# A convolution and attention kernel on one core: nine steps of the second image's statistics move from the fill into the first five periods, and two steps of offset arithmetic move ahead of a loop in the last period but one

## The chip, the core and the metric

The kernel runs on one core of one Trainium2 chip. A core has five engines, each with its own in-order queue of instructions: TensorE (PE, matrix products), VectorE (DVE), ScalarE (ACT), GpSimd (POOL) and SyncE (SP). [...] In this kernel SP issues most DMAs, POOL and ACT some. The metric is the device time of one execution in microseconds. The kernel before was run three times: 3306.95, 3310.23 and 3310.55 us, median 3310.23.

## What is computed

The input `x` has two images of 512 channels and 64 x 64 pixels. Two layers are applied, each of the form x + layer(groupnorm(x)), with 32 groups of 16 channels:

```
x = x + dcn(_gn(x))          # deformable convolution: offsets and mask from a depthwise
                             # 3x3 convolution, layer norm, Gelu and a product; bilinear
                             # sampling of a projected image; output projection
x = x + attention(_gn(x))    # q, k, v of all 4096 pixels, softmax, projection, batch norm, relu
```

The change is in the first layer. Its group norm needs mean and variance of every channel of an image before any pixel of that image can be normalized. Per image these are 32 statistics instructions (4 blocks of 128 channels, 8 pieces of 512 pixels), one aggregate for each block, and a short chain over the groups: product, differences, product, square root, reciprocal.

## The kernel before, in words

An image is cut into 8 chunks of 512 pixels (8 rows), and the two images make 16 chunks, 0 to 15. Each chunk passes through four stages, each written as a Python generator that issues some instructions and yields:

- `project` (L738): loads the chunk's rows, normalizes them on ACT (`xn`, L762), projects them on PE (`pq`, L772), and writes the result to DRAM (`xt`).
- `features` (L786): the depthwise convolution, 4 first taps on ACT (L798) and 32 taps on DVE (L806, about 0.7 us each), a sum over channels (`tot`, by POOL's DMAs and L816), the mean as a product (`p_mean`, L822), a subtraction (L827), squares on ACT (L832), the variance as a second product, the square root on ACT (`rstd`, L840), reciprocal and multiplication on DVE (L842, L843), and Gelu on ACT (L849).
- `weights` (L857): four pairs of a product `po` (L866) and an addition (L871), which are the first eight steps. Then, a step each: the exponential of the mask on ACT (L878); three operations on DVE that make `tx` from the offsets (L883, L884); a Relu on ACT (L890); the sums over the mask and its scaling on DVE (L893 to L898); the product `my` (L901); nine steps that add to `aw` (L909, L914); four copies to `at` on ACT (L919); and four transpositions `p_tr` with copies to `awT` (L928, L929).
- `sample` (L946): eight products `pb` with a copy to `bt` each (L957, L962), which for the last two chunks go to ACT and DVE by turns; eight groups of `pa` products with copies to `dT` (L976, L987); four output products `py` (L996), each followed by the residual's addition and a statistics instruction on DVE (L1001, L1002).

The order in which the four stages' steps are interleaved is written out by hand. Under `tc.manual_schedule()` each engine takes its instructions in the order in which the Python code issues them. First comes the fill, which brings chunks 0 to 2 under way: `p0`, `p1`, `p2` are their projections, `f0`, `f1`, `f` their features, and `v` the weights of chunk 0. Then come 16 periods. In period i, the function `period` (L1025) interleaves the end of the sampling of chunk i - 1 (`y`), the weights of chunk i + 1 (`w`), the sampling of chunk i (`m`), the features of chunk i + 2 (`f`, and `g` for the first step of the next) and the projection of chunk i + 3 (`p`); `v` is the tail of the weights of chunk i. `w(2)` issues two steps of `w`, and so on. Period 14 is `next_to_last`, period 15 `last_period`.

The statistics of the first image run at the very start. Those of the second are the generator `image_stats(1)` (L703), called `later`, and each `more()` issues one step of it. Its first step only issues three loads. Each of the next 32 steps issues, on POOL, the load of a piece two steps ahead (L714) and, on DVE, one statistics instruction (L727) on the piece that is due; after each eighth, an aggregate (L729) stands at the start of the next step. Five steps of the group norm follow (L598 to L616). The loads take turns in three pieces of memory, `early` (two) and `xraw` (one), so a load can be issued only when the statistics instruction three steps before the one that it feeds is done. Whatever is left is issued by `run(later)` ahead of period 5, which is the first to project a chunk of the second image.

Before the change, the fill calls `more()` 1, 6, 3 and 3 times and each period five times: once ahead of the features' taps and once after seven or so of their steps, once after the second of four groups of taps, once ahead of L842, and once at the end, after the last `aw` step. So the fill holds the first 12 statistics instructions, periods 0 to 3 hold five each, and period 4 and `run(later)` the group norm.

Of the kernel before, what the change touches and what calls it, by code (L numbers as in the profile page):

```python
# [533 lines left out]
@with_exitstack  # L534
def kernel(ctx: ExitStack, tc: tile.TileContext, t_in: dict, out: bass.AP):
    nc = tc.nc
    keep = ctx.enter_context(tc.tile_pool(name="keep", bufs=1))
    far = keep.tile([P, NSEQ], F32, name="far")
    sums = keep.tile([P, 2, 4 * G], F32, name="sums")
    nc.vector.memset(sums, 0.0)  # L540
    al = keep.tile([DQ, 2], F32, name="al_f")
    nc.gpsimd.dma_start(al[:, 0:1], t_in["L1_conv_align_w"])
    nc.vector.tensor_reduce(al[:, 1:2], al[:, 0:1], AX.X, ALU.max, apply_absolute_value=True)
    nc.vector.memset(al[:, 0:1], 1.0 / SCORE_MAX)
    beyond = keep.tile([1, 1], I32, name="beyond")
    again = window_path(tc, t_in, out, far, sums, al, beyond)

    with tc.If(again > 0):  # L550
        general_path(tc, t_in, out)
# [3 lines left out]
def window_path(  # L555
# [70 lines left out]
    with ExitStack() as l0:  # L626
# [68 lines left out]
        def border():  # L695
            for n in range(NB):
                for e in (0, 1, WIN - 2, WIN - 1):
                    nc.sync.dma_start(xt_d[n][e], edge[:WIN, :])
                    nc.sync.dma_start(xt_d[n][2 : H + 2, e, :], edge[:H, :])
# [234 lines left out]
        def fetch(i, s):  # L934

            if i >= NSEQ:
                return
            n, ch = divmod(i, NCH)
            t = io.tile([P, PX, C], F32, name="patch", bufs=2)
            for p in range(PX):  # L940
                nc.sync.dma_start(
                    t[:SN, p, :], xt_d[n][ch * ROWS + PR * s : ch * ROWS + PR * s + SY, PC * p : PC * p + SX, :]
                )
            patches[i, s] = t
# [61 lines left out]
        def run(*generators):  # L1006
            for gen in generators:
                for _ in gen:
                    pass
# [15 lines left out]
        def period(y, v, m, w, f, g, p, more, last, ahead, taps):  # L1025

            p()
            y()
            v(4)
            more()
            f(ahead)
            more()
            y()
            for k, count in enumerate(taps):
                m(2)
                w()  # L1040
                f(count)
                w()
                if k == 1:
                    more()
            w()
            m()
            w()
            m()
            f()
            y()  # L1050
            f()
            m()
            p()
            w(2)
            f()
            y(2)
            w()
            m()
            p()
            f()  # L1060
            w(2)
            p()
            y(2)
            more()
            f()
            y()
            m()
            p()
            for k, steps in enumerate((1, 2, 4, 0)):
                p()  # L1070
                w(steps)
                if k == 0:
                    if last:
                        m(3)
                    f()
                p()
                if k == 2:
                    more()
                if k < 3 and not last:
                    m()  # L1080
                if k == 0:
                    f()
                if k == 2:
                    g()
                    w(4)

        def next_to_last(y, v, m, w):

            y(3)
            w(8)  # L1090
            v(4)
            for steps, tiles in ((1, 2), (1, 2), (2, 1), (1, 0)):
                m(2)
                w(steps)
                y(tiles)
            for _ in range(4):
                m(2)
                w(2)
            w(5)
# [24 lines left out]
        def value_weights():  # L1124

            for cb in range(KB):
                pw = ps.tile([P, C], F32, tag="mm", name="pw")
                for kb in range(KB):
                    nc.tensor.matmul(
                        pw, wv[:, kb, cb * P : (cb + 1) * P], wf[kb], start=(kb == 0), stop=(kb == KB - 1)  # L1130
                    )
                t = io.tile([P, C], F32, tag="xj", name="wc_part", bufs=2)
                nc.scalar.copy(t, pw)
                nc.sync.dma_start(wc_d[:, cb, :], t)
                yield

        def output_bias():
            pb = ps.tile([P, C], F32, tag="mm", name="p_bias")
            for cb in range(KB):
                for kb in range(KB):  # L1140
                    nc.tensor.matmul(
                        pb[:, cb : cb + 1], out_w[:, kb, cb * P : (cb + 1) * P], in_b[:, kb : kb + 1],
                        start=(kb == 0), stop=(kb == KB - 1),
                    )
            nc.vector.tensor_add(out_b, out_b, pb[:, :KB])
            yield
# [4 lines left out]
        def more():  # L1151
            next(later, None)

        with tc.manual_schedule():

            p0, p1, p2 = [Chain(project, i) for i in range(3)]
            f0, f1, v, products = Chain(features, 0), Chain(features, 1), Chain(weights, 0), value_weights()
            p0()
            for kb in range(KB):
                p0()  # L1160
                f0()
            for t in range(4):
                p0(2)
                f0(8)
            border()
            more()
            p1()
            for kb in range(KB):
                p1()
                f1()  # L1170
                if kb == 1:
                    next(products)
                    next(products)
            f0()
            f1(5)
            p1(4)
            f0()
            f1(11)
            f0()
            for _ in range(6):  # L1180
                more()
            p1(4)
            f0(3)
            f1(16)
            next(products)
            fetch(0, 0)
            fetch(0, 1)
            p2()
            v(4)
            for _ in range(3):  # L1190
                more()
            f1()
            v(2)
            f1()
            v(2)
            p2(4)
            v()
            f1()
            v()
            f()  # L1200
            for _ in range(3):
                more()
            v(3)
            p2(4)
            f1()
            v(4)
            f1(2)
            v(5)
            p2(4)
            next(products)  # L1210
            run(output_bias())
            f(6)
            v(4)
            for i in range(NSEQ):
                if i == NCH - 3:
                    run(later)
                    for k, name in enumerate(("wkT", "wqT", "wkT")):
                        nc.sync.dma_start(wkq[:, :, k, :], t_in[name].rearrange("(kb p) m -> p kb m", p=P))
                    for h in range(2):
                        nc.sync.dma_start(al[h * DQ : (h + 1) * DQ, :], t_in["L1_conv_align_w"])  # L1220
                w, m, g = Chain(weights, i + 1), Chain(sample, i), Chain(features, i + 3)
                if i + 2 >= NSEQ:
                    (next_to_last if i + 1 < NSEQ else last_period)(y, v, m, w)
                    y, v = m, w
                    continue
                ahead, taps = (7, (9, 7, 6, 6)) if i else (0, (7, 7, 6, 6))
                period(y, v, m, w, f, g, Chain(project, i + 3), more, i + 3 == NSEQ, ahead, taps)
                y, v, f = m, w, g
            y.rest()
# [820 lines left out]
```

## Time and profile before

| | |
|---|---|
| median of three runs | 3310.23 us |
| the profiled execution | 3315.49 us |
| its span, first to last instruction | 3313.6 us |
| mean granted TensorE clock | 0.983 |
| VectorE's statistics instructions L727 (64, both images) | 0.674 to 0.696 us each |
| POOL's loads L714 for the second image | 256 KB each, 0.54 to 0.91 us of POOL, 2.9 to 6.9 us from issue to landing (those after 100 us) |
| first output product `py` of chunks 0, 1, 2, 3, 4 | 206.38, 273.6, 339.9, 405.68, 471.54 us |
| first output product of chunks 13, 14, 15 | 1054.74, 1112.27, 1153.38 us |

The second layer starts at 1168.17 us with its first product on PE. How to read the lines that the prediction shows: a timeline line has the start and the length in microseconds, the engine, the line of the kernel, the operation, what it writes and reads, the shapes, how many instructions were merged, and in brackets how long the engine had been idle before it and what ended that. The chain of waits is followed back from the last instruction: at each step to what released it, or to the instruction before it on its engine; its lines have start, length and what it was. An idle time counts only where its engine is on that chain.

### The profile page before, as it was taken

The numbers are of one execution on the slowest core, as the hardware profiler recorded it, in microseconds if no ns is written. First come the engines' busy times: TensorE is split into PE (matmuls) and PEld (weight loads), VectorE is DVE, ScalarE is ACT, GpSimd is POOL, SyncE is SP. The second block draws the span as 40 slices with busy tenths as digits, with TensorE's granted clock in tenths as the row PEclk, the third lists the DMA queues.
The fourth block names the chain that finished last, engine by engine and source line by source line (L and its number), as shares of the span: only waits on it lengthen the run. The fifth ranks groups of instructions, "written<-read, shape, count | busy, mean of one in ns | idle before, by whom it ended". The sixth has DMA issues, their size and how long they took to land.

```text
span 3313.6 us, 38405 instructions
## 1 busy us (share of the span) xinstructions
PE 3154.1 (95%) x14207; PEld 2264.5 (68%) x14207; DVE 2729.4 (82%) x3907; ACT 1343.0 (41%) x1848; POOL 292.0 (9%) x420
## 2 busy tenths in 40 slices
PE   4899999999999899999999999999999999999993
PEld 2455556555655667787787877887777787787782
DVE  7999999999998678995876977968897796886875
ACT  2678887888786533203113112023311202203114
POOL 1100000000000001001001011000001101001022
PEclk9999999999999999999999999999999999999997
DMA  6345443444343368748657677657677758648689
GB/s 238 120 117 155 151 129 109 137 146 118 109 136 124 115 236 282 220 154 242 189 174 212 197 203 204 199 185 251 226 213 200 205 181 234 199 160 238 194 320 373
DMA packets 241236, 629.06 MB, mean 190 GB/s; under 512 B 28528, under 2 KB 45552, under 8 KB 240016
## 3 DMA queue, kind: packets, MB, share of 16 engines
q1 hardware_dynamic: 177952, 413.37, 37.8%
q0 software_dynamic: 51936, 179.86, 20.7%
q10 hardware_dynamic: 11152, 33.30, 2.7%
q8 instruction: 114, 1.87, 0.2%
q14 instruction: 82, 0.67, 0.1%
HBM read 406.61 MB, written 124.91 MB: 160 GB/s over the span
## 4 chain that ended last, share of the span: by engine, by line
PE 79%; DVE 10%; ACT 5%; DMA 3%; issue 1%; SPq 1%; POOL 0%; ACTq 0%; POOLq 0%; DVEq 0%
PE accy L1572 21%; PE accx L1572 16%; PE pa L976 7%; PE py L996 6%; PE pS L1454 6%; PE pq L772 6%; PE po L866 4%; PE pvy L1809 3%; PE pvx L1809 2%; PE pk L1890 2%; PE pb L957 2%; ACT bt L962 1%; DMA tot<-e 1%; DVE conv L806 1%; PE p_mean L822 1%
## 5 line engine op out<-in xcount | busy, mean ns | idle before, releaser
L1572 PE MATMUL accy<-tt,v 128*128 128x256 f32 x1944 | 579.0, 379 | 0.7 <-DVE ct L1638 0.6
L1459 ACT ACTIVATE e<-pS 128x1024 f32<-128x1024 f32 x256 | 248.6, 1021 | 748.5 <-PE pS L1454 744.2
L1572 PE MATMUL accx<-e,v 128*128 128x256 f32 x1728 | 453.3, 385 | 0.0
L1572 PE MATMUL accy<-e,v 128*128 128x256 f32 x1728 | 443.4, 379 | 0.0
L1572 PEld LDWEIGHTS accy<-tt,v 128*128 128x128 f32 x1944 | 368.7, 190 | 53.3 <-DVE tt L1530 2.2
L806 DVE SCALAR_TENSOR_TENSOR conv<-xn,L_conv_dw_w_sb,conv 128x504 f32<-128x504 f32 (+1 forms) x512 | 376.7, 744 | 30.5 <-ACT conv L798 14.7
L1572 PEld LDWEIGHTS accx<-e,v 128*128 128x128 f32 x1728 | 320.5, 190 | 116.3 <-issue 77.4
L1572 PEld LDWEIGHTS accy<-e,v 128*128 128x128 f32 x1728 | 328.3, 190 | 44.6
L1530 DVE TENSOR_TENSOR tt<-tt,e 128x512 f32<-128x512 f32 x432 | 298.8, 692 | 14.8
L1572 PE MATMUL accx<-tt,v 128*128 128x256 f32 x972 | 289.4, 379 | 1.3 <-DVE tt L1529 1.3
L1529 DVE TENSOR_TENSOR tt<-e 128x256 f32<-128x256 f32 x432 | 180.7, 418 | 133.0 <-PE accy L1572 131.0
L976 PEld LDWEIGHTS pa<-bt,patch 96*128 96x128 f32 x2048 | 248.3, 195 | 57.1 <-issue 39.2
L976 PE MATMUL pa<-bt,patch 96*128 96x128 f32 x2048 | 252.3, 280 | 7.5 <-issue 4.0
L1454 PE MATMUL pS<-q,keys 64*128 64x512 f32 x1024 | 255.5, 616 | 1.1 <-DVE vform L1827 0.8
L962 ACT COPY bt<-pb 96x1024 f32<-96x1024 f32 x120 | 226.0, 2024 | 52.6 <-PE pb L957 52.6
L772 PE MATMUL pq<-in_w,xn 128*128 128x512 f32 x512 | 234.1, 600 | 3.5 <-ACT xn L762 3.5
L996 PE MATMUL py<-dT,L_conv_out_w_sb 128*128 128x512 f32 x512 | 230.0, 593 | 0.0
L1577 ACT COPY u<-accx 128x256 f32<-128x256 f32 x54 | 20.1, 372 | 474.5 <-PE accx L1572 471.7
L866 PE MATMUL po<-om_w_pg,feat 128*128 128x432 f32 x512 | 210.3, 557 | 0.8 <-ACT feat L849 0.8
L987 ACT COPY dT<-pa 32x256 f32<-32x256 f32 x496 | 179.9, 363 | 67.8 <-PE pa L976 59.0
L1572 PEld LDWEIGHTS accx<-tt,v 128*128 128x128 f32 x972 | 184.4, 190 | 27.6 <-DVE tt L1529 2.5
L996 PEld LDWEIGHTS py<-dT,L_conv_out_w_sb 128*128 128x128 f32 x512 | 95.5, 190 | 114.3 <-issue 107.6
(289 smaller groups left out, 4386.7 us busy)
## 6 DMA issues: line engine op xcount, KB each, us to landing
v<-wv SPq DMA_DIRECT2D x420, 448.0 KB
tot<-e POOLq DMA_DIRECT2D x160, 512.0 KB, 6.8
patch<-xt SPq DMA_DIRECT2D x256, 192.0 KB
wv<-vform SPq DMA_DIRECT2D x48, 512.0 KB
v<-ww SPq DMA_DIRECT2D x54, 448.0 KB
wv<-vsum SPq DMA_DIRECT2D x48, 384.0 KB
xt<-xj SPq DMA_DIRECT2D x128, 128.0 KB
res<-in_x SPq DMA_DIRECT2D x64, 256.0 KB
```

What stands on the lines that cost most here:

```text
L772: nc.tensor.matmul(pq, xn[:, kb, 1 + 2 * t : 3 + 2 * t, :].rearrange("p r c -> p (r c)"), in_w[:, kb, :], start=(kb == 0), stop=(kb == KB ...
L806: nc.vector.scalar_tensor_tensor(dst, src, wt, dst, ALU.mult, ALU.add)
L866: nc.tensor.matmul(po[:, : 3 * GP], f[:, kb, t * P : (t + 1) * P], om_w[:, kb].rearrange("p a k g -> p (a k g)"), start=(kb == 0), stop=(k ...
L962: copy(bt[:SN].rearrange("s g q d -> s d (g q)")[:, d0 : d0 + 4, :], pb[:SN])
L976: nc.tensor.matmul(pa[:, p], xp[:SN, p, cb * P : (cb + 1) * P], bt[:SN, 4 * cb : 4 * cb + 4, PX * s + p, :], start=True, stop=True,)
L987: copy(dst, src)
L996: nc.tensor.matmul(py, out_w[:, kb, cb * P : (cb + 1) * P], dT[:, kb, :], start=(kb == 0), stop=(kb == KB - 1))
L1454: nc.tensor.matmul(p[:, a, :], keys[r, i, (2 * u + h) * P : (2 * u + h + 1) * P], c.q[r, qh, :], start=True, stop=True,)
L1459: nc.scalar.activation(e.rearrange("p a q -> p (a q)"), p.rearrange("p a q -> p (a q)"), AF.Exp)
L1529: nc.vector.tensor_sub(t[:, 0], x[:, 1], x[:, 3])
L1530: nc.vector.tensor_add(t[:, 1:3], t[:, 0].unsqueeze(1).to_broadcast([P, 2, HQ]), x[:, 0:3:2])
L1572: nc.tensor.matmul(out, v[:, blk, :], op, start=(first and g == 0), stop=(final and g == NG))
```

## The change

In the fill, the six and the first three calls of `more()` are taken out; one before and three late in the fill stay. In `period`, a second call stands directly behind the first, ahead of the taps, and a second one directly behind that after the second group of taps. So the fill issues the first load step and 3 statistics instructions, the 35 calls of periods 0 to 4 issue the rest, and `run(later)` finds nothing left.

In `next_to_last`, the two steps of `w` that are the exponential and the `tx` operations are issued ahead of the loop over `m`, and the loop's third round issues none instead of two; the number of steps issued by the end of the loop is the same.

```
@@ period
             y()
             v(4)
             more()
+            more()
             f(ahead)
             more()
             y()
...
                 f(count)
                 w()
                 if k == 1:
+                    more()
                     more()
             w()
             m()
@@ next_to_last
             y(3)
             w(8)
             v(4)
-            for steps, tiles in ((1, 2), (1, 2), (2, 1), (1, 0)):
+            w(2)
+            for steps, tiles in ((1, 2), (1, 2), (0, 1), (1, 0)):
                 m(2)
                 w(steps)
                 y(tiles)
@@ the fill
             f0()
             f1(11)
             f0()
-            for _ in range(6):
-                more()
             p1(4)
             f0(3)
             f1(16)
...
             p2()
             v(4)
-            for _ in range(3):
-                more()
             f1()
             v(2)
             f1()
```

More of the change, by code (lines that the diff above doesn't have):

```diff
@@ L1034, in period @@
             more()
+            more()
             f(ahead)
@@ L1043, in period @@
                 if k == 1:
+                    more()
                     more()
@@ L1091, in next_to_last @@
             v(4)
-            for steps, tiles in ((1, 2), (1, 2), (2, 1), (1, 0)):
+            w(2)
+            for steps, tiles in ((1, 2), (1, 2), (0, 1), (1, 0)):
                 m(2)
@@ L1179, in window_path @@
             f0()
-            for _ in range(6):
-                more()
             p1(4)
@@ L1189, in window_path @@
             v(4)
-            for _ in range(3):
-                more()
             f1()
```

## The prediction

> **What bounds the kernel now.** I read the profiled execution top down: the page's busy times and chain, then the chain of waits in order of time for the three places that the change touches (the fill before about 143 us, periods 0 to 4 up to 471.5 us, the last period but one after 1054.7 us), then the timelines of single engines. "Period k" runs from where the last ends to its own end, by the first `py` product: 206.4, 273.6, 339.9, 405.7 and 471.5 us end periods 0 to 4.
>
> ```profile
> PE 3154.1 (95%) x14207; PEld 2264.5 (68%) x14207; DVE 2729.4 (82%) x3907; ACT 1343.0 (41%) x1848; POOL 292.0 (9%) x420
> PE 79%; DVE 10%; ACT 5%; DMA 3%; issue 1%; SPq 1%; POOL 0%; ACTq 0%; POOLq 0%; DVEq 0%
> ```
>
> TensorE carries four fifths of the chain. Whatever moves work on VectorE pays only where VectorE is in the other fifth. In the fill, the chain reads (start, us, what):
>
> ```profile
> 71.88 4.94 DMA wvfc<-wc_part
> 78.71 5.87 PE p_mean L822 x8
> 84.58 6.87 PE pq L772 x16
> 91.44 3.45 PE pw L1129 x8
> 94.92 3.49 ACT feat L849 x3
> ...
> 102.41 3.43 PE p_mean L822 x8
> 105.84 2.91 PE po L866 x8
> 108.75 0.02 issue
> 108.78 0.61 DVE o L871
> ```
>
> No `gn_st` is in it, although six stand on VectorE from 77.39 to 85.97 and three from 104.75 to 107.16. VectorE's timeline says why:
>
> ```profile
> 85.28 0.69 DVE L727 BATCH_NORM_STATS2 gn_st<-xraw 128x6 f32<-128x512 f32 x1 [1.44 <-DMA xraw<-in_x]
> 85.89 3.34 DVE L842 RECIPROCAL rstd<-rstd 128x512 f32<-128x512 f32 x1
> ...
> 108.78 0.61 DVE L871 TENSOR_TENSOR o<-po,om_b_pg 128x432 f32<-128x432 f32 x1 [1.61 <-PE po L866]
> ```
>
> The reciprocal at 85.89 needs ScalarE's `rstd`, written at 84.61 to 85.30; the three statistics ahead of 108.78 end 1.61 us before the product that is waited for. In period 0 and again in period 2 the chain does hold a statistic:
>
> ```profile
> 147.17 1.20 DVE gn_st L727 x2
> ```
> ```profile
> 292.09 0.69 DVE gn_st L727
> ```
>
> There VectorE is the bound, and TensorE waits at the mean (0.43 us at 170.71, 3.65 at 180.80, 0.37 at 303.06):
>
> ```profile
> 303.06 1.13 PE L822 MATMUL p_mean<-tot,ones_c 128*128 128x512 f32 x2 [0.37 <-DVE tot L816]
> ```
>
> **Part one, out of the fill.** Nine statistics go (0.684 us each, 0.60 start to start), with nine POOL loads of 256 KB (0.54 us of issue each) and one aggregate (0.37). The first six gone, the reciprocal starts at 85.35 instead of 85.89. But the Gelu behind it starts at 93.42 after a table load at 92.13, and that stands behind a ScalarE copy at 91.53 which waits for TensorE's `pq`; the reciprocal's successor L843 ended at 91.55, so 0.5 us earlier is no gain. The three at 104.75 only lengthen the wait of 1.61 us. If this cover were gone, VectorE would give back 9 x 0.60 + 4.64 us of DMA waits (2.79, 0.41, 1.44) = 10.0 us. I take 0, because the chain passes neither group; the bounds are 0 and -10.0. SP's queue is not passed by any of these loads.
>
> **Part one, into periods 0 to 4.** Each period gets a second step ahead of its taps and a second one after the second group of taps. In steps: 7 instead of 5 statistics in periods 0 to 3, one instead of none in period 4, where the group norm's steps follow.
>
> Period 0: VectorE has no idle time from 142.5 us to the subtraction at 174.02, where ScalarE's squares wait for it (1.55 us) and carry the chain on to 189.75. Both statistics are ahead: +2 x 0.60 = +1.2 us.
>
> Period 1: the first extra one falls into waits (0.64 for ScalarE's `conv` at 205.51, 0.82 for `py` at 210.01); the second eats from 1.45 us by which VectorE was early for the mean (TensorE free at 237.11, the total done at 235.66). TensorE stays +1.2; VectorE leaves at +1.8.
>
> Period 2: +0.60 ahead of the taps less the wait of 0.82 us for `py` at 277.28 (TensorE itself is +1.2 by then), then +0.60: without more, the total is +2.2 late, and as TensorE already waits 0.37 there, so is TensorE. But there is a new wait. The loads rotate through three pieces, so a statistic's load is issued only when the third before it is done. The steps now stand as last-of-period, first, second, four taps, third: the third's load starts behind the last-of-period's end and has about 4.25 us (two statistics at 0.60, four taps in 3.1). POOL issues 0.3 us after that end (271.45 + 0.68, issue at 272.43), and such loads took 4.5, 4.3 and 6.4 us from issue to landing at 204.57, 272.43 and 339.42:
>
> ```profile
> 339.42 0.54 POOL L714 DMA_DIRECT2D xraw<-in_x  x1 [18.00 <-DVE gn_st L727]
> ```
>
> The wait is 0.3 + (4.3 to 6.4) - 4.25 = 0.4 to 2.5 us each time; taps, residual add and the two taps groups stand behind it on VectorE, and the mean on TensorE waits for those. I take the middle, 1.4 in period 2 (period 1's has 4.5 and is covered by the `py` wait). TensorE: about +3.6 after period 2. Without the load's wait +2.2; with the long landing +4.6.
>
> Period 3: the wait for `py` is only 0.19 us (343.50) and the slack at the mean 0.08 (368.83 against 368.90). So 1.2 + a load wait of about 2.0 comes through nearly whole: TensorE +6.6 (bounds +3.1 and +8.2, by the same steps with no waits and with 6.4 us landings).
>
> Period 4: one statistic (0.60) goes into the `py` wait of 1.03 at 409.31. The norm's second product, which in the kernel before stood a step later (at 450.26), now directly follows the step that computes its operand, in TensorE's order ahead of the third group of `pb`:
>
> ```profile
> 421.72 1.13 PE L957 MATMUL pb<-awT,sel 25*96 25x256 f32 x16
> ```
> ```profile
> 424.11 0.16 DVE L604 TENSOR_TENSOR gn_d<-gn_d 128x4 f32<-128x4 f32 x1
> ```
>
> VectorE reaches that operand at 424.27, behind seven taps; TensorE would stand from 421.72: +2.6 us, and behind it `pb`, with ScalarE's copies waiting for it. TensorE has no other wait in the rest of the period that this could replace (0.23 us of slack at the mean). The norm's square root moves from the period's end (table load 1.28 and 1.10 us of waiting at 467.16) to beside the other square root at 449.87; TensorE had no gap after it, so 0.
>
> Clock: a short wait can cost more than itself. The windows show the granted clock at 0.50 from 1238 to 1242 us after a gap of 2.21 us at 1237.78, and at 0.91 in 540 to 560, in a period of 67.3 us (537.07 to 604.40) beside 65.5 (471.54 to 537.07) with the same waits of 0.83 and 0.46 to 0.48. So a dip costs about 1.7 us. Gaps of 1.76 and more were followed by one each time that I looked (1088.44, 1136.48, 1237.78); the 0.89 at 1168.17 was not. The 2.6 us in period 4 gets one: +1.7. Those at the mean in periods 2 and 3 may (0 to 1.7 each); a dip lost by a shift would be -1.7.
>
> [...]
>
> Part one: +6.6 + 2.6 + 1.7 = +10.9 us.
>
> **Part two, the last period but one.** The exponential and the three `tx` operations move ahead of the loop. The tx operations (2.8 us) fall into VectorE's wait of 3.18 us before 1077.21. The exponential on ScalarE then stands ahead of the first `bt` copy: its table load and 0.68 us end near 1077.9, that copy ends 0.8 us later, at 1079.9, before the next `pb` at 1080.66 needs its bank. Then every later VectorE step advances one place, and the third round has none:
>
> ```profile
> 1089.51 1.12 DVE L893 TENSOR_REDUCE sx<-o 128x64 f32<-128x576 f32 x1
> ...
> 1093.46 1.85 DVE L962 COPY bt<-pb 96x1024 f32<-96x1024 f32 x1
> ```
> ```profile
> 1095.41 17.03 PE L976 MATMUL pa<-bt,patch 96*128 96x128 f32 x128 [3.96 <-issue]
> ```
>
> TensorE stands 3.96 us until the last copy of `bt` ends (1095.31). With the sums (2.6 us) one round earlier, that copy starts when its `pb` is done, 1090.8 to 1091.5, and `pa` at 1092.75 to 1093.45: -2.0 to -2.7 us. I take -2.0, as the clock is at 0.50 there from 1090 on. What follows is bound by `pa` and passes it on.
>
> **Sum.** +10.9 - 2.0 = about +8 to +9; I take +8, a little under, as the dip's chance is not 1. The profiled execution took 3315.49 us (span 3313.6 and 1.9 around it), 5.3 over the median of 3310.23; on it the sum gives 3323.5, on the median 3318. Ends of this case: no load waits and no dips, 3.1 + 2.6 - 2.7 = +3.0; long landings and two dips, 8.2 + 2.6 + 3.4 - 2.0 = +12.2. A measurement here can tell about 0.2%, 6.6 us.
>
> **Rivals.**
> *The periods hide it.* TensorE's periods without these statistics (65.5 us) are as long as those with five (65.8), which speaks for spare VectorE time; the slacks of 0.08 and -0.31 at the mean speak against. Only part two and half of the wait in period 4 would be left: -2.0 to +0.6, about 3309.5.
> *The fill is VectorE's after all* (faster). VectorE is at 90% in it, and 10.0 us leave; it needs the copy of `xj` at 91.53 to come earlier than `pq` allows. With the periods hiding theirs: -12, 3298. It decides from 6.6 us of the 12.
> *The POOL queue spreads the delay.* Every added load stands on the queue that also carries `tot` accumulations (3.3 us to landing); the total at 302.32 has some 2 us left. If two periods lose 2 to 3 us there on top: +14 or more, 3326.
>
> **How the numbers follow.** Forecast 0.65 (its ends +3.0 and +12.2 are 3313.2 and 3322.4; the bound 3310.23 + 6.6 = 3316.8 leaves 5.6 of these 9.2 us, 0.6, above it), hidden 0.17, faster fill 0.10, POOL 0.08. Slower: 0.65 x 0.6 + 0.08 = 0.47; faster 0.10; same, the rest, 0.43. The range leaves out the fill's and POOL's cases: 3307 to 3323.
>
> **What would show it.** Right: `gn_st` alone at 115 us in the fill and the `at` copies at the same 142.7 us; the mean of period 0 some 1.2 us later; VectorE waiting for `early` or `xraw` ahead of the third statistic; a TensorE wait of about 2.6 us for `gn_d`; `pa` two us closer to its `pb` in the last period but one. Wrong: `at` copies well before 142.7, or means that come on time in periods 2 and 3.

## The result, and the profile after

The changed kernel takes 3323.32 us (median of six runs, 3321.33 to 3329.76), the kernel before 3310.39 (six runs, 3306.95 to 3313.31). The ratio is 1.0037, with an interval from 1.0028 to 1.0047, so 9 to 16 us slower. The prediction said 3318, slower, in a range from 3307 to 3323: the sign came out, and the mechanism in the main; the size was too small, with the measured time at the range's upper end.

The profiled execution of the changed kernel took 3322.75 us with a span of 3320.7. The page's first lines:

```profile
PE 3152.9 (95%) x14207; PEld 2265.5 (68%) x14207; DVE 2729.9 (82%) x3907; ACT 1341.7 (40%) x1847; POOL 292.4 (9%) x420
PE 72%; DVE 12%; DMA 6%; ACT 4%; issue 4%; SPq 1%; POOL 0%; ACTq 0%; POOLq 0%; DVEq 0%
```

The engines are as busy as before. What changed is the chain: TensorE's share fell from 79 to 72%, and DMA rose from 3 to 6%. The table sets the profiled executions side by side, period by period (us, from one chunk's first `py` to the next; the first row is the start of the first `p_tr`). The three columns on the right are experiments that are told below.

| | before | after | part one alone | norm apart | late instead |
|---|---|---|---|---|---|
| fill | 143.68 | 143.29 | 143.55 | 142.50 | 142.80 |
| period 0 (from `p_tr`) | 62.70 | 63.74 | 63.25 | 63.76 | 63.19 |
| period 1 | 67.26 | 66.41 | 66.41 | 66.40 | 66.40 |
| period 2 | 66.22 | 69.31 | 70.56 | 69.76 | 67.12 |
| period 3 | 65.82 | 69.01 | 68.29 | 69.12 | 67.25 |
| period 4 | 65.86 | 71.46 | 68.46 | 65.66 | 65.90 |
| periods 5 to 13, with dips of the clock | 583.2 | 578.1 | 583.2 | 583.3 | 578.2 |
| period 14 | 57.53 | 56.07 | 57.55 | 56.29 | 56.13 |

A dip of the granted clock (to 0.50, for 3.41 us in these periods) makes an otherwise equal period 1.4 to 1.7 us longer (67.3 instead of 65.6 in most). The profiled execution of before had one in period 1 and four in periods 6 to 13, that of after one there. Mainly for that reason the two spans lie only 7.1 us apart, and the medians 12.9.

In the fill next to nothing is gained: in the four executions with the changed fill it ends at 142.50 to 143.55 us, in the two with the fill of before (one is the second part alone, told below) at 143.68 and 143.95. VectorE's timeline of the changed kernel, where the nine statistics are gone:

```profile
84.78 3.36 DVE L842 RECIPROCAL rstd<-rstd 128x512 f32<-128x512 f32 x1 [7.40 <-ACT rstd L840]
...
108.23 0.61 DVE L871 TENSOR_TENSOR o<-po,om_b_pg 128x432 f32<-128x432 f32 x1 [4.48 <-PE po L866]
```

What was work is now waiting. The reciprocal starts when `rstd` is there, and the addition when its product is, as before.

In period 0 TensorE now waits 1.62 us at the mean, where it waited 0.43 before (the first line is the kernel before):

```profile
170.71 1.13 PE L822 MATMUL p_mean<-tot,ones_c 128*128 128x512 f32 x2 [0.43 <-DVE tot L816]
```
```profile
171.36 1.13 PE L822 MATMUL p_mean<-tot,ones_c 128*128 128x512 f32 x2 [1.62 <-DVE tot L816]
```

In the periods the chain of waits now names the moved steps and their loads (start, us, what):

```profile
146.63 1.79 DVE gn_st L727 x3
...
159.88 1.19 DVE gn_st L727 x2
```
```profile
273.39 5.97 DMA early<-in_x
...
342.30 6.06 DMA xraw<-in_x
```

VectorE waits for a load, in front of the residual's addition, in periods 2 and 3 (2.11 and 1.66 us):

```profile
279.38 0.69 DVE L727 BATCH_NORM_STATS2 gn_st<-early 128x6 f32<-128x512 f32 x1 [2.11 <-DMA early<-in_x]
279.99 0.73 DVE L1001 SCALAR_TENSOR_TENSOR res<-py,L_conv_out_b_sb,res 128x512 f32<-128x512 f32 x1
...
348.38 0.69 DVE L727 BATCH_NORM_STATS2 gn_st<-xraw 128x6 f32<-128x512 f32 x1 [1.66 <-DMA xraw<-in_x]
```

and TensorE waits for that addition (2.44 us in period 2, 2.14 in period 3), then in period 4 for the norm's operand:

```profile
280.78 0.66 PE L928 MATMUL p_tr<-ident,at 128*128 128x128 f32 x4 [2.44 <-DVE res L1001]
...
349.79 0.66 PE L928 MATMUL p_tr<-ident,at 128*128 128x128 f32 x4 [2.14 <-DVE res L1001]
```
```profile
430.40 0.59 PE L607 MATMUL gn_p<-gn_d,gmat_sb 128*128 128x4 f32 x2 [2.54 <-DVE gn_d L604]
430.92 2.05 PE L957 MATMUL pb<-awT,sel 25*96 25x256 f32 x16
432.90 5.11 PE L866 MATMUL po<-om_w_pg,feat 128*128 128x432 f32 x8
```

The `po` group behind the wait took 5.11 us instead of 3.17: the clock was halved there, from 430.03 to 436.86 us (third column from the end: the granted clock):

```profile
430.03:436.86 6.83, 6.46 (x24) 3.59 (x25) 4.58 (x8) 3.71 (x2) 0.86 (x1) 0.50 0.22 38
436.86:440.27 3.41, 3.41 (x24) 1.69 (x23) 2.15 (x4) 1.18 (x1) 0.00 (x0) 1.00 0.00 0
```

In period 14 the gap ahead of `pa` went from 3.96 to 2.01 us:

```profile
1100.08 17.45 PE L976 MATMUL pa<-bt,patch 96*128 96x128 f32 x128 [2.01 <-issue]
```

### The profile page after: what moved, and what is told of

It is laid out like the page before. It is cut to its first block, busy times and chain, and to the rows that moved or that the text cites. A ratio compares the mean times of both kernels' runs of the same rounds, so it can differ in the third digit from the quotient of the medians.

```text
span 3320.7 us, 38410 instructions
## 1 busy us (share of the span) xinstructions
PE 3152.9 (95%) x14207; PEld 2265.5 (68%) x14207; DVE 2729.9 (82%) x3907; ACT 1341.7 (40%) x1847; POOL 292.4 (9%) x420
## 4 chain that ended last, share of the span: by engine, by line
PE 72%; DVE 12%; DMA 6%; ACT 4%; issue 4%; SPq 1%; POOL 0%; ACTq 0%; POOLq 0%; DVEq 0%
PE accy L1571 21%; PE accx L1571 16%; PE pS L1453 6%; PE pa L976 6%; PE py L996 6%; PE pq L772 5%; PE po L866 3%; DVE conv L806 3%; PE pvy L1808 2%; PE pvx L1808 2%; PE pk L1889 2%; DMA tot<-e 2%; PE pb L957 1%; ACT bt L962 1%; DVE tt L1529 1%
```

## The experiments

My theory was: the fill hides what is taken out of it, periods 0 to 3 lose by VectorE's load and by waits for loads, period 4 by one product that stands right behind its operand, and period 14 gains 2 us. The rivals were that VectorE's load alone makes the periods long, that the fill gains, and that period 14's gain is lost later. The prediction also had a rival in POOL's queue, where the added loads delay the partial sums of `tot`. It needs no run of its own: the third of these DMAs took 3.24 to 3.29 us to land in periods 0 to 4 of the kernel before and 3.27 to 3.38 in the changed one, and in neither does VectorE wait for them ahead of the total (L816). Each ratio is to the kernel before, run on the same chip.

**The second part alone.**

```
-            for steps, tiles in ((1, 2), (1, 2), (2, 1), (1, 0)):
+            w(2)
+            for steps, tiles in ((1, 2), (1, 2), (0, 1), (1, 0)):
```

> The kernel before with the second part of the change alone (the exponential and the tx steps ahead of the loop in period 14). By my theory the last copy of bt is made earlier and TensorE's gap ahead of pa shrinks from 3.96 to about 2.0 us, and the second layer passes that on: 2.0 us less than before, 3308.4 us, ratio 0.9994. By the rival, that something later (the second layer's first loads) takes it back: 1.000. If it cost time on ScalarE: above 1.0005.

Measured: 1.0000 (0.9991 to 1.0009). The gap ahead of `pa` is 2.01 us here too, and period 14 takes 56.28 us instead of 57.53:

```profile
1086.64 17.81 PE L976 MATMUL pa<-bt,patch 96*128 96x128 f32 x128 [2.01 <-issue]
```

So the trace shows 1.3 us and the times can't tell 1.3 us from none. Of the 1.95 us that the gap lost, the `pa` group gave some back: it runs 0.8 us longer (17.81 instead of 17.03), as more of it falls under the halved clock (6.5 instead of 4.9 us). No cost on ScalarE shows in the period. Nor does a later place take the gain back, as far as the traces tell: from the end of period 14 to the end of the span, the five executions with the second part take 2201.0 to 2203.3 us, the three without it 2201.3 to 2204.7.

**The first part alone**: the changed kernel with that loop as before.

> The changed kernel with period 14 as before, so the moved statistics alone. By my theory nothing is gained in the fill (its end, the first p_tr, within 0.6 us of 143.7) and periods 0 to 4 lose about 1.0, 0.7, 3, 3 and 5.6 us: 13 to 15 us above before, about 3324 us, ratio 1.0042. By the rival, that the fill gains and a part of the loss comes from period 14: under 1.0030.

Measured: 1.0042 (1.0028 to 1.0055), 3324.97 us. The loss is that of the moved steps; by the times, none of it comes from period 14. This run also prices the wait in period 4 by itself, since the clock did not dip behind it:

```profile
430.70 0.39 PE L607 MATMUL gn_p<-gn_d,gmat_sb 128*128 128x4 f32 x2 [2.52 <-DVE gn_d L604]
431.02 1.13 PE L957 MATMUL pb<-awT,sel 25*96 25x256 f32 x16
432.08 3.17 PE L866 MATMUL po<-om_w_pg,feat 128*128 128x432 f32 x8
```

The windows from 420 to 440 us of the changed kernel and of this one (the granted clock again third from the end):

```profile
420.00:440.00 20.00, 17.00 (x75) 8.54 (x75) 16.17 (x26) 11.92 (x7) 2.30 (x3) 0.83 0.36 101
```
```profile
420.00:440.00 20.00, 17.00 (x81) 8.52 (x79) 19.09 (x31) 15.00 (x9) 2.30 (x3) 1.00 0.38 106
```

Period 4 takes 68.46 us here, 2.6 over the 65.86 of before: the wait itself. With the dip it takes 71.46, 3.0 more: that dip lasted 6.83 us, where those of periods 2 and 3 lasted 3.41. Period 2 lost more here (70.56), with a wait of 3.35 us for its load.

**The norm's product apart from its operand.**

```
-                if k == 1:
-                    more()
+                if k in (1, 2):
                     more()
```

> The changed kernel with the second of the two steps after the second group of taps moved behind the third group, in all periods, so that in period 4 the norm's second product no longer stands right behind its operand; periods 0 to 3 have as many statistics ahead of the mean as in the changed kernel. By my theory TensorE's wait of 2.54 us for gn_d and the dip of the clock behind it go: period 4 takes 66 to 67.5 us instead of 71.5, the kernel 4 to 5.5 us less than the changed one, about 3318.5 us, ratio 1.0025. By the rival, that VectorE's load makes period 4 long, it stays at 70 us or more and the ratio at 1.0037.

Measured: 1.0018 (1.0009 to 1.0027), 3317.42 us; the changed kernel's interval, 1.0028 to 1.0047, lies just above this one. Period 4 is back at 65.66 us, with its statistics and the norm still in it, and the product no longer waits:

```profile
428.65 3.17 PE L866 MATMUL po<-om_w_pg,feat 128*128 128x432 f32 x8
431.65 0.28 PE L607 MATMUL gn_p<-gn_d,gmat_sb 128*128 128x4 f32 x2
431.86 1.81 PE L957 MATMUL pb<-awT,sel 25*96 25x256 f32 x16
```

Periods 2 and 3 are as in the changed kernel (69.76 and 69.12). So period 4's loss was the place of one product that takes 0.28 us, with the dip of the clock behind it, and not VectorE's load.

**The extra step behind the mean instead of ahead of the taps.**

```
             v(4)
             more()
-            more()
             f(ahead)
...
             y(2)
             more()
+            more()
             f()
```

> The changed kernel with the extra step ahead of the taps moved to a place after the mean (doubling the step ahead of the reciprocal L842). Each period has as many steps as in the changed kernel, but the last step of a period, and the two ahead of and among the taps, are no longer four in a row, so no statistic should wait for its load; in period 4 the norm's product falls away from its operand as well. By my theory (the wait for loads) periods 2 and 3 go from 69.3 and 69.0 us to 66.3 to 67.5, period 4 to about 66, and the kernel to about 3311.5 us, ratio 1.0003 (up to 1.0010 with dips of the clock). By the rival (VectorE's load of seven statistics a period alone) periods 2 and 3 stay above 68.3 us and the ratio is 1.0020 or more.

Measured: 1.0011 (1.0002 to 1.0020), 3314.72 us; the profiled run 3309.98. Periods 2 and 3 take 67.12 and 67.25 us, although each still has seven statistics. The third statistic of period 2 starts without a wait, and TensorE's wait at `p_tr` shrinks to 0.25 us:

```profile
273.17 3.07 DVE L806 SCALAR_TENSOR_TENSOR conv<-xn,L_conv_dw_w_sb,conv 128x504 f32<-128x504 f32 x4
276.16 0.69 DVE L727 BATCH_NORM_STATS2 gn_st<-early 128x6 f32<-128x512 f32 x1
```
```profile
277.55 0.66 PE L928 MATMUL p_tr<-ident,at 128*128 128x128 f32 x4 [0.25 <-DVE res L1001]
```

So 2.2 us of period 2's loss and 1.8 of period 3's went, most of it the wait for loads with the dip behind it. This edit also takes one statistic (0.60 us) from ahead of the mean, so up to 0.6 us of each may be VectorE's load and not the loads' wait; no run separates the two. What is left, 0.9 and 1.4 us over the kernel before, is VectorE's load: TensorE's waits at the mean are 0.90 us in both periods, where the kernel before had 0.37 and none. The rival holds for that part of the loss: 0.9 to 1.5 of 3.1 us in period 2 and 1.4 to 2.0 of 3.2 in period 3.

**Nine statistics left out.** The kernel before, without the nine that the change takes out of the fill and without their loads. A constant stands in their place, so the second image is normalized with wrong figures; the rest of the computation is there.

```
+            if n:
+                for _ in range(9):
+                    pieces.popleft()
+                nc.gpsimd.memset(mv, 1.0)
...
-            for _ in range(6):
-                more()
...
-            for _ in range(3):
-                more()
```

> The kernel before with nine of the second image's 32 statistics, those that the change takes out of the fill, left out altogether (no load, no statistic; a constant stands in their place, so the second image is normalized with wrong figures); the periods and period 14 are as before. By my theory the fill hides all nine: the first p_tr comes 0 to 0.6 us earlier and the time is 3310 us, ratio 0.9995 to 1.0005. By the rival that VectorE is the fill's bound, 10 us go: 3300 us, ratio 0.997.

Measured: 0.9998 (0.9989 to 1.0007), 3312.02 us beside 3312.74. The fill ends at 144.12 us instead of 143.68. VectorE only waits:

```profile
85.86 3.35 DVE L848 RECIPROCAL rstd<-rstd 128x512 f32<-128x512 f32 x1 [7.57 <-ACT rstd L846]
...
109.31 0.61 DVE L877 TENSOR_TENSOR o<-po,om_b_pg 128x432 f32<-128x432 f32 x1 [4.49 <-PE po L872]
```

Ten microseconds of work and waits were taken from VectorE's timeline and the fill gave back none. That rival falls.

**The other way.** The second part, with one more statistic in the fill and, in period 0, one ahead of the mean and two behind it, instead of three and one.

```
             f0(3)
+            more()
             f1(16)
...
             f(ahead)
-            more()
+            if ahead:
+                more()
...
-                if k == 1:
+                if k == 1 and ahead:
                     more()
...
             y(2)
             more()
+            if not ahead:
+                more()
```

> The second part of the change, with statistics moved the other way: one more in the fill, ahead of the 16 taps of the second chunk, where VectorE has about 1.1 us to spare before the mean; in period 0 one step ahead of the mean instead of three, and two instead of one ahead of the reciprocal, where VectorE waits 1.05 us for rstd. Periods 1 to 4 are as before. By my theory period 0 gets 1.2 us shorter (from 62.7 us after the first p_tr to 61.5) and period 14 by 2.0: 3307.2 us, ratio 0.9990. By the rival, that the fill is VectorE's bound or period 0 is TensorE's, 0.9994 or above.

Measured: 0.9989 (0.9980 to 0.9998), 3308.4 us beside 3312.74: below the kernel before, and below the changed one. But it isn't the reason that I gave. Period 0 took 63.07 us from the first `p_tr`, not 61.5. With two statistics fewer ahead of it, VectorE now waited for a product:

```profile
154.76 0.61 DVE L871 TENSOR_TENSOR o<-po,om_b_pg 128x432 f32<-128x432 f32 x1 [1.36 <-PE po L866]
```

The `pb` and `po` groups ahead of it took 2.05 and 4.33 us instead of 1.14 and 3.17, because the clock, at 0.50 ahead of the first `p_tr` in both, came back at 152.70 us here and at 147.96 in the kernel before. So VectorE's freed 1.2 us went into a wait for TensorE, and what they are worth at a full clock isn't shown. What this kernel gained in its profiled run is period 14 (54.63 us, with the same gap of 2.01 us and 6.83 us of halved clock instead of 10.24) and dips: one in periods 5 to 13 instead of four (578.1 instead of 583.2 us) and none in period 1. How much of the ratio is the second part and how much the dips stays open: its interval overlaps that of the second part alone.

## Why the prediction was right or wrong

- *Out of the fill, 0.* Right. The fill ended 0.4 us earlier with the change (up to 1.5 by the other executions, of the 10.0 that left VectorE) and 0.4 later with the nine left out, and the chain in the fill is the one that the prediction read, product by product.
- *Period 0, +1.2.* Right: +1.04. TensorE's wait at the mean went from 0.43 to 1.62 us. (The second part alone, with period 0 as before, took 62.31 us; the first part alone and the run with the norm apart, with period 0 as changed, 63.25 and 63.76.)
- *Period 1, 0.* Too low. The 1.45 us of slack that I counted was owed to a dip of the clock in that very period of that one execution: with the second part alone, where period 1 is the same and has no dip, the total is done at 235.22 us and TensorE free at 235.28, a slack of 0.06. An undisturbed period 1 takes 65.81 us (the second part alone) and took 66.41: +0.6, with a wait at the mean of 0.54 us.
- *Periods 2 and 3, +2.4 and +3.0.* The size was near (+3.1 and +3.2) and the cause right: loads of 6.0 and 6.1 us on the chain, waits of 2.11 and 1.66 us against 1.4 and 2.0. The place was wrong. I had the mean on TensorE wait; it waited earlier, at the last of the four `p_tr` groups (2.44 and 2.14 us, both ended by `res` of L1001), whose place in PSUM is free only when L1001 has read the `py` that was in it. I had looked at the addition as a place where VectorE waits, and not asked who waits for it. The waits at the mean in these periods were 0.04 and 0.10 us. The nearness of the sizes is in part luck: all of TensorE's waits together grew by 2.2 us in period 2 and 2.3 in period 3, and the remaining 0.9 of each is products slowed by a dip, which the prediction's 2.4 and 3.0 did not hold.
- *Period 4, +2.6 and a dip of 1.7.* The wait was 2.54 us, and 2.52 with the first part alone. The dip was under-sized: it cost 3.0 us and not 1.7, so the period lost 5.6, not 4.3. It lasted 6.83 us, twice the 3.41 of those from which the 1.7 was worked out, and ScalarE's copies of `bt` came late behind the slowed products (a wait of 0.72 us for them at 442.89).
- *Dips.* One was in the sum. The changed kernel had three: at 283 and 352 us, behind its new waits of 2.44 and 2.14 us, and at 430 us, 0.37 us before the end of the one of 2.54. This is the term that was mis-sized. In the clock's records of the kernel before and of the changed one, every dip but the last, which runs to the end, is to 0.50 and lasts 3.41 us or a whole multiple (6.83, 10.24), and all begin whole multiples of 3.413 us apart (20 and 23 between those at 283.26, 351.52 and 430.03 us). In period 4 of the changed kernel one such step fell at 430.03 us, with 2.17 us of the wait ahead of it; with the first part alone one fell at 430.05, carried on from that trace's earlier dips, with 1.86 us ahead of it, and the clock did not dip (1.00 from 420 to 440 us). So the wait that reached further ahead of its step had the dip; two cases give no threshold.
- *Part two, -2.0.* The gap shrank by 1.95 us, the period by 1.3 to 1.5.
- *The sum.* By the traces, with period 1 taken undisturbed, periods 0 to 4 lost 1.0 + 0.6 + 3.1 + 3.2 + 5.6 = 13.5 us and period 14 gave back 1.5: +12.0, or +11.6 with the 0.4 us of the fill, beside +12.9 between the medians. Against the +10.9 and -2.0 of the prediction, period 4 (1.3), period 2 (0.7), period 1 (0.6) and period 14 (0.5) make the difference, less 0.2 in period 0 and plus 0.2 in period 3. I took +8 on top of that "as the dip's chance is not 1"; that shaving went the wrong way.

## What to carry to other kernels

Work that stands on a busy engine in a stage is not thereby the stage's bound: follow the chain through the stage, and if the work isn't in it, taking it out gives next to nothing (here 0.4 us of the fill for the 10.0 that left VectorE), while the place to which it goes may have no room. When steps are doubled, look at what pairs of neighbours they make: a load that is issued by the step three before it, or a product right behind the operand that another engine makes, can cost more than the steps themselves (waits of 1.66 to 2.54 us here, beside 0.60 us for a statistic and 0.28 for the product), and one step's distance took that cost away. A slack read from one execution should be read in a second execution, or in a second period of the same kind, since a dip of the clock can make it (in period 1, 1.45 us with a dip and 0.06 without).

## What was not expected of the hardware

Short waits of TensorE were followed by the halved clock (0.50) more often than I had thought: in the changed kernel, the first part alone and the run with the norm apart, every wait at `p_tr` in periods 2 and 3 (1.42 to 3.69 us, six of them) was followed by one within the next products, and of the two waits of 2.5 us in period 4 one was.

Nor does it take such a wait. Of the 23 periods (1 to 13 of the kernel before, 1 and 5 to 13 of the changed one) whose longest wait of TensorE is 0.83 us or less, 6 had a dip. They differ in place: carry the 3.413 us grid of each trace through these periods, and a step of it falls 1.19 to 1.75 us behind the start of the `pb` products that follow the wait of 0.45 to 0.48 us for `bt` in all 6 periods with a dip, and in none of the 17 without (the nearest are 1.17 and 1.90 us). In periods 5 to 13, the same code in both, the kernel before had four dips and the changed one had one.

The loads of 256 KB that POOL issues at the turn into period 2 took 6.0 to 8.4 us to land in the three executions where it issues three of them in a row, and 4.3 to 6.6 in the five where it issues two. At the turn into period 3 the ranges overlap (5.3 to 7.6 and 5.8 to 6.9 us).
